# Sums of |w| gathered before one small product, an earlier statistics merge and a split last block in a four-layer convolution kernel

## The chip, the core and the metric

The kernel runs on one core of a Trainium2 chip. The metric is the device time of one execution in microseconds (us). The kernel before took 1045.62 us, the median of 10 runs, which lie between 1042.13 and 1047.35 us.

## The reference: what is computed

The input is a batch of 16 images with 256 channels of 28 x 28 pixels, in float32. Four layers follow each other:

```
layer 0: binarised input, 3x3 convolution with sign-like weights, batch norm, residual
layer 1: sign, 3x3 convolution with real weights, norm, gates, then a 1x1 convolution, gates
layer 2: batchnorm -> sign -> conv(w1) -> prelu -> batchnorm -> sign -> conv(w2) -> prelu -> batchnorm -> + x -> prelu
         conv weights are  mean(|w|) * sign(w)
layer 3: attention over the 784 pixels of each image, projection, + x
```

Two things matter here. The three binary convolutions (one in layer 0, two in layer 2) multiply signs by signs, so they are run with the bare signs, and the scale `mean(|w|)` per output channel enters later, in the normalisation. And the batch norm behind each of them needs the mean and variance of every channel over all 16 images, so nothing after it can start before the last image has been convolved.

## The kernel before, in words

**A binary convolution** is the function `sign_layer`. It is called three times: for layer 0 (its statistics are called `l0`, written `l_` in the profile), and for the two convolutions of layer 2 (`l2b` and `l2c`). An image is cut into two halves of 14 rows x 28 columns = 392 pixels, so there are 32 blocks, numbered `j`. For each block TensorE does 18 matmuls (2 groups of input channels x 9 taps), each with its own 128x128 weights (L285). The two halves of the output channels are packed into one number (`PACK` = 4095), and the function `apart` takes them apart again: two passes on ScalarE (L294, L295) and one on VectorE (L296). The function `post` then works on the block: in layer 0 two `bn_stats` on VectorE (L515) and a conversion to int16 on ScalarE (L516); in layer 2 for each half of the channels a PReLU (L1016) and a `bn_stats` (L1017) on VectorE, and a square on ScalarE (L1019) that watches the range.

**The order** is written out by hand in the loop of `sign_layer`, and each engine works through its part of it in that order. Iteration `j` issues: the products of block `j`; on even `j` the signs of the next image on ScalarE (L390, L982); `post` of block `j - 1`; at `j = 30` the early merge of the statistics; the second part of the previous step (`late`); the first part of the next step; `apart` of block `j`. The products may run ahead of the rest by as many blocks as PSUM has tiles for them, which is three (`ps_conv`, bufs=3).

**Steps** are pieces of work for later layers, put between the blocks. In layer 0 they are, from `j = 2`: six `w1_step` (weights of layer 1) alternating with six `add_up` for layer 0's own weights (odd `j`, 3 to 13), then one step for the 1x1 weights, one for constants, and from `j = 16` to 21 six combined steps for the first weights of layer 2. In the first convolution of layer 2 there is a step that starts loads and then, at `j = 3` to 8, six combined steps for the second weights. A combined step takes the signs of a chunk of weights on ScalarE (L231), packs them on VectorE in its late part (L232), and adds up |w|: `add_up` reduces the chunk to 256 sums per partition on VectorE (L239); its late part, `total_up`, sums those over the partitions with two float32 products with a vector of ones on TensorE (L245; four matmuls in the profile) and adds the result to the scale on VectorE (L247 for the first chunk, L249 for the others). The signs go to a tile with one buffer (`sg`; two in layer 0's own).

**Statistics.** `Moments` holds the `bn_stats` of the blocks. Those of the first 29 blocks go to `parts` and are merged by `gather` (L154, L155) in iteration 30; the last three go to `fin`, beside the merged entry, and a second merge (L171) over 21 numbers per channel half gives mean and variance. `norm` turns them into scale and shift.

**Dummy products.** `keep_busy(n)` issues `n` bf16 products of 512 columns on TensorE whose result nobody reads (L371), to keep its clock up. They stand between the layers, in TensorE's order.

A second version of the whole computation (`careful`) is in the program, but is run only when a check of the ranges asks for it.

Of the kernel before, what the change touches and what calls it, by code (L numbers as in the profile page):

```python
# [28 lines left out]
F32 = mybir.dt.float32  # L29
# [10 lines left out]
P = 128  # L40
# [3 lines left out]
HN = N // 2  # L44
HR = S // 2
K9 = 256 * 9
MC = 112
GN, GC = N // 4, MC // 4
NC_ = N // MC
# [27 lines left out]
def forward(ctx: ExitStack, tc: tile.TileContext, d: dict, out: bass.AP, careful: bool):  # L77
# [16 lines left out]
    def pv(name):  # L94
        return vec[:, VECS.index(name), :]
# [15 lines left out]
    for t, c in ((rounding, ROUND), (unrounding, -ROUND)):  # L111
        nc.gpsimd.memset(t, c)

    doubts = const.tile([P, 8 * B + 6], F32, name="doubts")
    nc.gpsimd.memset(doubts, 0.0)

    def vtile(name):
# [99 lines left out]
    def sign_weights(pool, dst, src, total, acc, stage=("st", 2), tmp=None, ab_tag="rn", sg=("sg", 1)):  # L217


        sts = {}  # L220
        tmp = tmp or pool

        def load(k, g):
            if (k, g) not in sts:
                sts[k, g] = load_taps(pool, src, k, g, *stage)

        def sign(k, g):
            st = sts[k, g]
            n = CHUNKS.index((k, g))
            t = tmp.tile([P, 3, 256], BF16, tag=sg[0], name="sg", bufs=sg[1])  # L230
            A.activation(t, st, AF.Sign, saturate=False)  # L231
            return lambda: V.scalar_tensor_tensor(  # L232
                dst[:, n], t[:, :, P:], PACK, t[:, :, 0:P], ALU.mult, ALU.add
            )

        def add_up(k, g):
            st = sts.pop((k, g))
            ab = tmp.tile([P, 256], F32, tag=ab_tag, name="ab", bufs=4 if ab_tag == "rn" else 2)
            V.tensor_reduce(ab, st.rearrange("p t o -> p o t"), AX.X, ALU.add, apply_absolute_value=True)  # L239
            return lambda: total_up(k, g, ab)  # L240

        def total_up(k, g, ab):
            part = acc.tile([P, 2], F32, tag="sm", name="sumabs")
            for mo in range(2):
                T.matmul(part[:, mo:mo + 1], lhsT=ab[:, mo * P:(mo + 1) * P], rhs=ones, start=True, stop=True)  # L245
            if k == 0 and g == 0:
                V.tensor_scalar(total, part, 1.0 / K9, None, ALU.mult)  # L247
            else:
                V.scalar_tensor_tensor(total, part, 1.0 / K9, total, ALU.mult, ALU.add)  # L249

        return [[Step(lambda c=c: load(*c), lambda c=c, f=f: f(*c)) for c in CHUNKS] for f in (sign, add_up)]

# [14 lines left out]
    def sign_layer(pads, w, temp, sign, post, steps, moments, together=1):  # L267

        pss = [None] * 2 * B
        abs_ = [None] * 2 * B

        groups = 2 if careful else 1
        size = 6 // groups

        def products(*js):
            for j in js:
                pss[j] = conv_ps()
            for n, (k, g) in enumerate(CHUNKS):  # L280
                for j in js:
                    for t in range(3):
                        r, c = divmod(3 * g + t, 3)
                        r += HR * (j % 2)
                        T.matmul(  # L285
                            pss[j][:, n // size, :HN].rearrange("p (a b) -> p a b", b=S), lhsT=w[:, n, t, :],
                            rhs=pads[:, j // 2 % 2, k, r:r + HR, c:c + S],
                            start=(n % size == 0 and t == 0), stop=(n % size == size - 1 and t == 2),
                        )

        def apart(j):
            for g in range(groups):
                t, ab, ps = temp("t1"), temp(), pss[j][:, g, :HN]
                A.activation(t, ps, AF.Identity, bias=rounding, scale=1.0 / PACK)  # L294
                A.activation(ab[:, 1], t, AF.Identity, bias=unrounding)  # L295
                V.scalar_tensor_tensor(ab[:, 0], ab[:, 1], -PACK, ps, ALU.mult, ALU.add)  # L296
                if g == 0:
                    abs_[j] = ab
                else:
                    tt(abs_[j], abs_[j], ab, ALU.add)  # L300

        def sign_image(i):

            for r0, r1 in ((0, HR + 1), (HR + 1, S)) if i < together else ((0, S),):
                sign(i, slice(r0, r1), lambda k: inner(pads[:, i % 2], k, r0, r1))

        late = None
        with tc.manual_schedule(engines={ET.PE, ET.Activation, ET.DVE, ET.SP}):
            sign_image(0)
            for j in range(2 * B):  # L310
                if j == 0:
                    products(*range(together))
                elif together <= j:
                    products(j)
                if j % 2 == 0 and j // 2 + 1 < B:
                    sign_image(j // 2 + 1)
                if j > 0:
                    post(j - 1, abs_[j - 1])
                if j == 2 * B - 2:
                    moments.gather()  # L320
                if late:
                    late()
                late = steps.pop(0)() if j >= 2 and steps else None
                apart(j)
            post(2 * B - 1, abs_[2 * B - 1])
        assert not steps and not late

    def inner(pad, k, r0=0, r1=S):
# [8 lines left out]
        V.tensor_scalar(v, a, f, c, ALU.mult, ALU.add)  # L337
        return v


    def halves_moments(name):
        return Moments(name, 2 * B - 3, 3, (2 * B - 3) * HN)

    sf0, sf1, sf2 = vtile("sf0"), vtile("sf1"), vtile("sf2")
    w0 = packed_weights(wpool, tag="wa")
# [13 lines left out]
    with tc.tile_pool(name="ps_conv", bufs=3, space=PSUM) as psc, \  # L359
# [7 lines left out]
        def keep_busy(n):  # L367

            ps = pss.tile([P, 512], F32, tag="sm", name="unused")
            for _ in range(n):  # L370
                tc.keep_in_program_order(T.matmul(ps, lhsT=idle[:, 0:P], rhs=idle, start=True, stop=True))  # L371

        with tc.tile_pool(name="ph1", bufs=1) as ph:
# [20 lines left out]
            def temp(tag=None):  # L394
                if tag:
                    return ph.tile([P, HN], F32, tag=tag, name=tag, bufs=2)
                return ph.tile([P, 2, HN], F32, tag="rn", name="ab", bufs=4)
# [72 lines left out]

            def constants():
                nc.gpsimd.tensor_copy(
                    doubts[:, 8 * B:], vec[:, VECS.index("a1"):VECS.index("a3") + 1, :].rearrange("p i k -> p (i k)")
                )
                v = const.tile([P, 4, 2], F32, name="v_bn")
                for i, bn in enumerate(bns):
# [31 lines left out]
            steps.insert(13, constants)  # L508

            def post0(j, ab):  # L510
                b, h = divmod(j, 2)
                if h == 0:
                    ns[b] = ph.tile([P, 2, N], I16, tag="n", name=f"n{b}", bufs=2)
                for mo in range(2):
                    V.bn_stats(mom.part(j, mo), ab[:, mo])  # L515
                A.copy(ns[b][:, :, h * HN:(h + 1) * HN], ab)  # L516
                if h == 1:
                    nc.gpsimd.dma_start(out=n0d[b], in_=ns[b])

            mom = halves_moments("l0")  # L520
            sign_layer(fpads, w0, temp, sign0, post0, steps, mom, together=2)
            for b in range(2):
                xs[b] = None
# [347 lines left out]

            with tc.manual_schedule(engines={ET.PE, ET.DVE, ET.Activation}):
                sc0, bi0 = norm("l0", mom, pv("g0"), pv("b0"), sf0, first)
                mom.doubt(doubts[:, 0:4 * B])
                zb1 = tt(vtile("zb1"), bi0, pv("a_move"), ALU.add)
                sign1(0, 0)
                enter(0, 1, sc0)
# [89 lines left out]
        with tc.tile_pool(name="ph2", bufs=1) as ph:  # L967
# [4 lines left out]
                shape = [P, 2, HN] if tag == "ab" else [P, HN]  # L972
                return ph.tile(shape, F32, tag=tag, name=tag, bufs=3 if tag == "ab" else 2)

            keep_busy(12)


            order = [B - 3, B - 2, B - 1] + list(range(B - 3))
# [22 lines left out]
            def post2(order, alpha, mom, doubt):  # L1001

                if careful:
                    beta = combine(mom.name + "_beta", alpha, -1.0, 1.0)

                def post(j, ab):
                    i, h = divmod(j, 2)
                    for mo in range(2):
                        y = ab[:, mo]
                        p = pt[order[i]][:, mo, h * HN:(h + 1) * HN]  # L1010
                        if careful:
                            r = temp("t1")
                            A.activation(r, y, AF.Relu, scale=-1.0)
                            V.scalar_tensor_tensor(p, r, beta[:, mo:mo + 1], y, ALU.mult, ALU.add)
                        else:
                            V.scalar_tensor_tensor(p, y, alpha[:, mo:mo + 1], y, ALU.mult, ALU.max)  # L1016
                        V.bn_stats(mom.part(j, mo), p)  # L1017
                    if not careful:
                        A.activation(temp("t2"), ab[:, 0], AF.Square, scale=SAFE**-0.5, accum_out=doubt[:, j:j + 1])  # L1019
                return post  # L1020

            steps = both(*sign_weights(xpool, w2b, d["w2b"], sf2, pss, ("x2", 3), tmp=ph, ab_tag="sums"))
# [1 line left out]
            def first_loads(some=steps[:2]):  # L1024
                for s in some:
                    s.load()

            steps = [first_loads] + load_ahead(steps, 2, now=False)
            mom = halves_moments("l2b")
            sign_layer(fpads, w2a, temp, sign2a, post2(order, pv("a1"), mom, doubts[:, 4 * B:6 * B]), steps, mom)  # L1030

            keep_busy(30)
            sg2, bg2 = norm("l2b", mom, pv("g2"), pv("b2"), sf1)

            mom = halves_moments("l2c")
            sign_layer(
                fpads, w2b, temp, lambda i, rows, out: sign2(pt[i], sg2, bg2, rows, out),
                post2(range(B), pv("a2"), mom, doubts[:, 6 * B:8 * B]), [], mom,
            )

            keep_busy(45)
# [550 lines left out]
```

## Time and profile before

| | |
|---|---|
| median of 10 runs | 1045.62 us |
| the profiled execution's own time | 1043.47 us |
| its span (first to last instruction) | 1041.7 us |
| granted TensorE clock, mean | 0.991 |
| layer 0, to TensorE's first product of layer 1 | 139.3 us |
| layer 1, to the first product of the first convolution of layer 2 | 139.3 to 514.5 us |
| first convolution of layer 2, to the first product of the second | 514.5 to 640.2 us |
| second convolution of layer 2, to the end of its normalisation | 640.2 to 757.1 us |
| attention and output | to 1041.7 us |

In the profile PE is TensorE's matmuls, PEld its weight loads, DVE is VectorE, ACT is ScalarE, POOL is GpSimd and SP the queue that issues most transfers. A group of instructions is named by line, engine, operation and by what it writes and reads. [...] A matmul's end is modelled, and its duration (356 ns) is longer than the distance from one to the next: block 10 to block 31 of the first convolution of layer 2, 396 matmuls, go from 557.18 to 632.13 us, which is 0.189 us each, or 3.41 us for a block.

### The profile page before, as it was taken

How to read it: one execution, taken by the hardware profiler on the slowest of the kernel's cores; microseconds unless marked ns; L12 is line 12 of the kernel's file. 1: busy time of each engine (PE TensorE's matmuls, PEld its weight loads, DVE VectorE, ACT ScalarE, POOL GpSimd, SP SyncE). 2: the span in 40 equal slices, each digit the busy share in tenths (PEclk: the TensorE clock that was granted, in tenths of full speed). 3: DMA queues.
4: the chain of work that ended last, by engine and by line, in shares of the span. 5: the costliest groups of instructions: out<-in, count | busy, mean ns of one | idle time of the engine just before them, and what ended most of it. 6: DMA issues, size and time to landing. Idle time of an engine off the chain costs nothing.

```text
span 1041.7 us, 15026 instructions
## 1 busy us (share of the span) xinstructions
PE 1007.0 (97%) x5667; PEld 827.4 (79%) x5667; DVE 826.1 (79%) x1460; ACT 729.7 (70%) x1189; POOL 139.4 (13%) x147
## 2 busy tenths in 40 slices
PE   7999999999999999999999999999999999999995
PEld 6899979999999999997589997999844444444442
DVE  4987588999999999985688887888865777768765
ACT  7888746777777777775777775777676676766652
POOL 2000100000000000000100000000024344443531
PEclk9999999999999999999899999999999999999998
DMA  9755521222332223100464000000023435344312
GB/s 345 232 190 189 198 78 47 93 78 78 109 109 93 78 78 107 64 32 31 182 256 180 1 1 1 2 1 1 1 35 59 101 86 124 70 118 92 95 63 97
DMA packets 24358, 98.77 MB, mean 95 GB/s; under 512 B 3202, under 2 KB 6980, under 8 KB 24276
## 3 DMA queue, kind: packets, MB, share of 16 engines
q1 hardware_dynamic: 18644, 67.17, 18.4%
q0 software_dynamic: 5632, 30.54, 10.9%
q8 instruction: 47, 0.77, 0.3%
q14 instruction: 35, 0.29, 0.1%
HBM read 65.59 MB, written 32.11 MB: 94 GB/s over the span
## 4 chain that ended last, share of the span: by engine, by line
PE 82%; DVE 9%; ACT 6%; issue 1%; DMA 1%; SPq 0%; POOL 0%; ACTq 0%; POOLq 0%; DVEq 0%
PE cv L614 27%; PE cv L285 23%; PE sc L1218 8%; PE av L1239 8%; PE cv L720 4%; PE mi L1195 4%; PE sm L1281 2%; PE mi L1297 2%; DVE ab L296 1%; ACT ab L295 1%; DVE p L1016 1%; PE unused L371 1%; ACT t L294 1%; PE sm L1239 1%; DVE l_parts L515 1%
## 5 line engine op out<-in xcount | busy, mean ns | idle before, releaser
L285 PE MATMUL cv<-fpads,wpk 128*128 128x392 f32 x1728 | 336.2, 356 | 9.0 <-POOL l_fin L152 7.3
L285 PEld LDWEIGHTS cv<-fpads,wpk 128*128 128x128 f32 x1728 | 327.2, 192 | 11.8 <-POOL l_fin L152 7.3
L614 PE MATMUL cv<-vs,w 128*128 128x392 f32 x1536 | 301.0, 354 | 1.4 <-DVE vs L121 1.4
L614 PEld LDWEIGHTS cv<-vs,w 128*128 128x128 f32 x1536 | 287.0, 190 | 3.1 <-issue 1.8
L1222 ACT ACTIVATE es<-sc 128x784 f32<-128x784 f32 x112 | 87.3, 822 | 41.4 <-PE sc L1218 41.4
L296 DVE SCALAR_TENSOR_TENSOR ab<-ab,cv 128x392 f32<-128x392 f32 x96 | 53.9, 561 | 65.4 <-ACT ab L295 65.1
L1218 PE MATMUL sc<-q,keyswa 64*128 64x392 f32 x448 | 89.9, 513 | 0.9 <-ACT es L1222 0.9
L1016 DVE SCALAR_TENSOR_TENSOR p<-ab,vec 128x392 f32<-128x392 f32 x128 | 79.1, 618 | 2.2
L1239 PE MATMUL av<-es,v 128*64 128x392 f32 x448 | 80.7, 499 | 0.0
L294 ACT ACTIVATE t<-cv,rounding 128x392 f32<-128x392 f32 x96 | 55.4, 577 | 26.9 <-PE cv L285 25.6
L1218 PEld LDWEIGHTS sc<-q,keyswa 64*128 64x128 f32 x448 | 38.9, 186 | 44.0 <-issue 17.1
L1232 POOL TENSOR_TENSOR sum<-sum,es 128x784 f32<-128x784 f32 x32 | 67.3, 2102 | 3.1 <-ACT es L1222 0.6
L1239 PEld LDWEIGHTS av<-es,v 128*64 128x64 f32 x448 | 29.4, 136 | 47.3 <-issue 47.0
L121 DVE TENSOR_TENSOR vs<-pad 128x840 fp32r<-128x840 bf16 (+1 forms) x66 | 64.5, 1001 | 0.1
L295 ACT ACTIVATE ab<-t,unrounding 128x392 f32<-128x392 f32 x96 | 59.8, 623 | 3.2
L1206 DVE COPY keyswa<-mi 64x392 f32<-64x392 f32 x31 | 16.3, 564 | 52.2 <-ACT q L1202 52.2
L760 POOL DMA_DIRECT2D x2d<-x x16 | 8.6, 536 | 359.5 <-DVE x L754 296.9
L1019 ACT ACTIVATE t<-ab 128x392 f32<-128x392 f32 x64 | 33.5, 523 | 26.6 <-DVE ab L296 26.6
L720 PE MATMUL cv<-z,fw 128*128 128x392 f32 x256 | 48.8, 341 | 0.7 <-ACT z L712 0.7
L737 ACT ACTIVATE u<-cv,c_bn,s_bn 128x784 f32<-128x784 f32 x30 | 30.2, 1005 | 24.4 <-PE cv L720 24.4
L720 PEld LDWEIGHTS cv<-z,fw 128*128 128x128 f32 x256 | 45.8, 188 | 1.5 <-ACT z L712 1.3
L1195 PE MATMUL mi<-p,wqk 128*128 128x392 f32 x124 | 45.3, 506 | 0.3 <-PE unused L371 0.2
(275 smaller groups left out, 1500.3 us busy)
## 6 DMA issues: line engine op xcount, KB each, us to landing
xs<-in_x_dram SPq DMA_DIRECT2D x30, 784.0 KB, 4.9
x2d<-x POOLq DMA_DIRECT2D x16, 784.0 KB, 3.6
out_dram<-p SPq DMA_DIRECT2D x15, 784.0 KB, 3.7
p<-x2d POOLq DMA_DIRECT2D x14, 784.0 KB, 6.9
p<-x2d SPq DMA_DIRECT2D x13, 784.0 KB, 6.7
n0d<-n POOLq DMA_DIRECT2D x16, 392.0 KB, 5.0
n<-n0d SPq DMA_DIRECT2D x16, 392.0 KB, 3.1
st<-in_w_dram SPq DMA_DIRECT2D x12, 384.0 KB, 6.2
```

Source lines behind the costliest of these rows:

```text
L121: V.tensor_tensor(o, a, b, op)
L285: T.matmul(pss[j][:, n // size, :HN].rearrange("p (a b) -> p a b", b=S), lhsT=w[:, n, t, :], rhs=pads[:, j // 2 % 2, k, r:r + HR, c:c + S] ...
L294: A.activation(t, ps, AF.Identity, bias=rounding, scale=1.0 / PACK)
L295: A.activation(ab[:, 1], t, AF.Identity, bias=unrounding)
L614: T.matmul(ps.rearrange("p (a b) -> p a b", b=S), lhsT=w[:, k, c, u, mo * P:(mo + 1) * P], rhs=vs[:, b % 2, u, k, :, c:c + S], start=(n == 0),
L720: T.matmul(ps[:, h, :HN], lhsT=w[:, k, mo * P:(mo + 1) * P], rhs=z2[b][:, k, h * HN:(h + 1) * HN], start=(k + i == 0), stop=(k + i == 2),)
L1016: V.scalar_tensor_tensor(p, y, alpha[:, mo:mo + 1], y, ALU.mult, ALU.max)
L1195: T.matmul(ps[:, h, :HN], lhsT=wqk[:, k, :], rhs=x[b][:, k, h * HN:(h + 1) * HN], start=(k == 0), stop=(k == 1))
L1218: T.matmul(ps[:, h, :HN], lhsT=chunk[rows], rhs=qs[b][rows], start=True, stop=True)
L1222: A.activation(e, ps[:, :, :HN], AF.Exp, scale=0.125)
L1232: (V if late else nc.gpsimd).tensor_tensor(sums[b, late], sums[b, late], e, ALU.add)
L1239: T.matmul(ps[64 * h:64 * h + 64, :HN], lhsT=w, rhs=e[:, h, :], start=start, stop=stop)
```

## The change

There are three parts, and one number.

1. The |w| sums of all six chunks are added on VectorE into one tile of 256 columns (the first chunk is reduced straight into it, each other chunk is reduced into its own tile and then added), and only after the last chunk the two small products sum it over the partitions. So each of the three weight sets has one group of small products instead of six, and five additions of 128x256 on VectorE.
2. The early merge of the statistics covers the first 26 blocks and is issued in iteration 27. The later merge then covers the merged entry and seven blocks, 45 numbers.
3. The last block of 14 rows becomes two of 7 rows, 196 pixels each, so that there are 33 blocks; `products`, `apart` and the `post` functions take the rows of a block from a list.
4. The 12 dummy products ahead of layer 2 become 6.

```
+BLOCKS = [(j // 2, HR * (j % 2), HR) for j in range(2 * B - 1)] + [(B - 1, r, HR // 2) for r in (HR, HR + HR // 2)]
+NB = len(BLOCKS)
+EARLY = 26
...
         def add_up(k, g):
             st = sts.pop((k, g))
-            ab = tmp.tile([P, 256], F32, tag=ab_tag, name="ab", bufs=4 if ab_tag == "rn" else 2)
+            if not all_:
+                all_.append(tmp.tile([P, 256], F32, tag="total", name="sums", bufs=1))
+                ab = all_[0]
+            else:
+                ab = tmp.tile([P, 256], F32, tag=ab_tag, name="ab", bufs=4 if ab_tag == "rn" else 2)
             V.tensor_reduce(ab, st.rearrange("p t o -> p o t"), AX.X, ALU.add, apply_absolute_value=True)
-            return lambda: total_up(k, g, ab)
-
-        def total_up(k, g, ab):
+            if ab is not all_[0]:
+                tt(all_[0], all_[0], ab, ALU.add)
+            return total_up if (k, g) == CHUNKS[-1] else lambda: None
+
+        def total_up():
             part = acc.tile([P, 2], F32, tag="sm", name="sumabs")
             for mo in range(2):
-                T.matmul(part[:, mo:mo + 1], lhsT=ab[:, mo * P:(mo + 1) * P], rhs=ones, start=True, stop=True)
-            if k == 0 and g == 0:
-                V.tensor_scalar(total, part, 1.0 / K9, None, ALU.mult)
-            else:
-                V.scalar_tensor_tensor(total, part, 1.0 / K9, total, ALU.mult, ALU.add)
+                T.matmul(part[:, mo:mo + 1], lhsT=all_[0][:, mo * P:(mo + 1) * P], rhs=ones, start=True, stop=True)
+            V.tensor_scalar(total, part, 1.0 / K9, None, ALU.mult)
...
+                    i, r0, rows = BLOCKS[j]
                     for t in range(3):
                         r, c = divmod(3 * g + t, 3)
-                        r += HR * (j % 2)
+                        r += r0
                         T.matmul(
-                            pss[j][:, n // size, :HN].rearrange("p (a b) -> p a b", b=S), lhsT=w[:, n, t, :],
-                            rhs=pads[:, j // 2 % 2, k, r:r + HR, c:c + S],
+                            pss[j][:, n // size, :rows * S].rearrange("p (a b) -> p a b", b=S), lhsT=w[:, n, t, :],
+                            rhs=pads[:, i % 2, k, r:r + rows, c:c + S],
...
-            for j in range(2 * B):
+            for j in range(NB):
...
-                if j == 2 * B - 2:
+                if j == EARLY + 1:
                     moments.gather()
...
-        return Moments(name, 2 * B - 3, 3, (2 * B - 3) * HN)
+        return Moments(name, EARLY, NB - EARLY, EARLY * HN)
...
-            keep_busy(12)
+            keep_busy(6)
```

The remaining lines give the same row ranges to `apart` and the `post` functions, and widen the tile of the range checks from 134 to 138 columns.

## The prediction

> **What bounds the kernel now.** I read the page's chain of waits first (TensorE 82%, VectorE 9%, ScalarE 6%), then who waited for whom on TensorE, then the timeline around the |w| sums and at the ends of the three binary convolutions.
>
> The waits, as the change sees them: TensorE sat 7.3 us ahead of the small products.
>
> ```profile
> PE sumabs L245 <- DVE ab L239: 7.3, 10, 1.4
> ```
>
> The timeline of one combined step in layer 0: signs of weights (L231), `apart` (L294, L295, L296), statistics, packing (L232), then the next signs.
>
> ```profile
> 86.49 1.03 DVE L239 TENSOR_REDUCE ab<-st 128x256 f32<-128x768 f32 x1
> 86.54 0.84 ACT L231 ACTIVATE sg<-st 128x768 bf16<-128x768 f32 x1
> 87.29 0.57 ACT L294 ACTIVATE t<-cv,rounding 128x392 f32<-128x392 f32 x1
> 87.64 0.52 PEld L245 LDWEIGHTS sumabs<-ones,ab 128*128 128x128 f32 x4 [0.41 <-PE cv L285]
> ...
> 87.89 0.62 ACT L295 ACTIVATE ab<-t,unrounding 128x392 f32<-128x392 f32 x1
> ...
> 88.55 0.56 DVE L296 SCALAR_TENSOR_TENSOR ab<-ab,cv 128x392 f32<-128x392 f32 x1 [1.03 <-ACT ab L295]
> 89.14 1.04 DVE L515 BATCH_NORM_STATS2 l_parts<-ab 128x6 f32<-128x392 f32 x2
> ...
> 90.10 0.54 DVE L232 SCALAR_TENSOR_TENSOR wpk<-sg 128x384 fp32r<-128x384 bf16 x1
> 90.56 0.15 DVE L249 SCALAR_TENSOR_TENSOR sf<-sumabs,sf 128x2 f32<-128x2 f32 x1
> 90.63 1.03 DVE L239 TENSOR_REDUCE ab<-st 128x256 f32<-128x768 f32 x1
> 90.67 0.84 ACT L231 ACTIVATE sg<-st 128x768 bf16<-128x768 f32 x1 [0.69 <-DVE wpk L232]
> ```
>
> From signs to signs is 90.67 - 86.54 = 4.13 us, and no member of that ring is on TensorE: 0.75 to L294, 0.60 to L295, 0.66 to L296, 0.59 to the statistics, 0.96 to L232, 0.57 to the next L231. TensorE needs 18 x 0.19 = 3.42 for its block and 0.44 for the small products. It isn't the bound here: it is dragged by the reduction, which ends at 87.52. In the first convolution of layer 2 the ring is 5.46 us long (L296 at 535.79, 541.25, 546.71, 552.16), and TensorE idles more.
>
> The clock, in stretches of 3.41 us there (columns: us, then busy of PE, PEld, DVE, ACT, POOL, granted clock, DMA): after 2.06 us busy of 3.42 it was halved for just such a stretch.
>
> ```profile
> 544.95:548.36 3.41, 2.54 (x15) 2.56 (x16) 2.31 (x4) 2.31 (x5) 0.00 (x0) 1.00 1.02 425
> 548.36:551.78 3.42, 2.06 (x14) 1.73 (x12) 2.74 (x6) 1.59 (x3) 0.00 (x0) 1.00 1.01 420
> 551.78:555.19 3.41, 3.41 (x12) 3.41 (x12) 2.92 (x6) 2.73 (x5) 0.00 (x0) 0.50 1.02 423
> ```
>
> The end of that convolution: the early merge holds VectorE from 629.71, so `apart` of block 30 starts at 631.56 though ScalarE was done at 630.21.
>
> ```profile
> 629.71 1.72 DVE L154 BATCH_NORM_AGGREGATE l2b_fin<-l2b_parts 128x2 f32<-128x174 f32 x2
> 631.47 0.17 DVE L155 TENSOR_SCALAR l2b_fin<-l2b_fin 128x2 f32<-128x2 f32 x1
> 631.56 0.56 DVE L296 SCALAR_TENSOR_TENSOR ab<-ab,cv 128x392 f32<-128x392 f32 x1
> ```
>
> **The change, part by part.** All sums are differences to the profiled execution (1043.47 us; span 1041.7 and 1.8 around it). It is 2.15 under the median, so I add the difference to the median.
>
> *Additions on VectorE, layer 0's own weights (odd j, 3 to 13).* Here the reduction ends just as ScalarE does: 43.16 + 1.02 = 44.18, L295 ends at 44.20, L296 starts at 44.23, and the chain runs on through VectorE (statistics, L249 0.06, `w1_step`). An addition of 128x256 is the row `asm` of L121: 0.43, of which the next instruction overlaps 0.1. So each of the additions of chunks 2 to 6 delays L296 by 0.31; the sixth passes on 0.26 (ScalarE's signs hide 0.05). Five L249 or L247 go at 0.06: 4 x 0.31 + 0.26 - 0.30 = **+1.2**.
>
> *Additions in the combined steps.* VectorE idles 1.03 ahead of L296 (second fence); 0.45 fits. Cost 0; without that idle time ten of them would cost 4.5.
>
> *TensorE's small products.* 15 of 18 groups go, 0.44 each, but the steps where they stood are paced by the rings, so nothing is won there. The last group stays, between the products of blocks 22 and 23 (9 and 10 in layer 2), and now waits for reduction and addition. Queued behind it is everything TensorE has left of the layer, and from there on the chain is TensorE alone. Addition +0.45, less one L249 of 0.06: **+0.37** in layer 0, **+0.34** in layer 2. The transfers keep their places in SP's and POOL's queues.
>
> *The clock at that wait.* Freed of the other waits, TensorE runs ahead until PSUM's three tiles stop it: block j starts when L296 of block j - 3 ends. In layer 2, block 9 starts at 547.3 (L296 of block 6), ends at 550.7, and the last small products come at 557.15: 6.4 us without work, so the clock is halved when block 10 starts. It stays so until a stretch is mostly busy, some 3.4 us (1.7 to 5.1 by the phase), which costs half: **+1.7** (0 to 2.6), passed on whole, since TensorE then bounds 22 blocks. In layer 0, blocks 20 to 22 come early likewise; L296 of block 19 ends at 93.2, block 22 at about 98 by the queue, the wait lasts to 100.5, and with the 0.44 of near-empty products that makes 2.9 us. A stretch loses over 1.4 of it in most phases: **+1.4** (0 to 2.5).
>
> [...]
>
> *Dummy products, 12 to 6.* They end at 514.52, while ScalarE's first signs (L982 from 512.00, 0.73 each with 0.1 overlap) are there at about 513.3 for both channel groups. TensorE's later dummies lie 0.215 apart at full clock: 6 x 0.215 = 1.29, and conv would start at 513.23, about when its data is there. **-1.3**, passed on through the ring. Ends: 0 (if the clock falls) and -1.3.
>
> *Earlier merge.* 156 numbers at iteration 27 cost 1.6 of VectorE, which gains 3.42 - 2.95 = 0.47 a block in layer 2: absorbed by block 31. In layer 0 VectorE idles 1.8 a block. The last merge grows from 21 to 45 numbers: (902 - 246) / 153 = 4.3 ns each, +0.1 for the one on the path.
>
> *The split block.* No fp32r product of 196 columns is in the trace. Weight loads of 128 columns alone follow each other at 0.11 (four in 0.52, one of them 0.19); a product of 392 takes 0.19. Lower end 0.098 (half of 0.196), upper end 0.354, the float32 rate (L1195, 8 matmuls in 2.83; a product is two of them, at half the columns each). I take 0.11, the row with the same weights and few columns. Then TensorE ends 36 x 0.11 - 3.42 = 0.54 later. VectorE's instruction of 196 columns is L1269: 360 against 625, so 0.265 less each; ScalarE's loses 0.17 (L1173, 1037 to 703 for 392). End of the first convolution of layer 2: without the merge, L296 of block 30 at 630.25, VectorE free at 633.12, quarter one's L296 there, its square on ScalarE at 633.46, quarter two's L294 at 633.93, L295 634.38, L296 634.87, last statistics end 636.53, mean and variance at 636.94 instead of 637.69: **-0.75**. The second convolution has the same end: **-0.75**. In layer 0 the merge hid already; quarter two's L294 waits for the int16 copy of quarter one and starts at 132.36, L296 at 133.30, result 134.59 instead of 134.67: **-0.1**. The 30 dummies behind end 0.54 later and still ahead of the next product.
>
> Sum: 1.2 + 0.37 + 1.4 - 0.1 + 0.34 + 1.7 - 1.3 - 0.75 - 0.75 = **+2.1**, so 1045.6 + 2.1 = 1047.7.
>
> **Rivals.**
>
> *TensorE's queue sets the steps after all* (faster). For it: the chain runs through the small products, 0.60 + 0.38 + 4 x 0.58 in layer 0 and 0.58 + 0.51 in layer 2. Against it: the ring adds up to 4.13 without them. If true, 2.9 and 0.65 go, and TensorE never idles long enough to lose its clock: 2.1 - 2.9 - 0.65 - 3.1 = -4.5, 1041.1. It is faster by the bound once TensorE keeps its clock (-3.1), layer 2 gains its 0.65 and the ring of layer 0 falls under 4.05 us (six steps, -0.45).
>
> *A product of 196 columns costs as much as one of 392* (0.19). TensorE's end comes 3.4 later in each convolution; the tails become +2.4, +1.9 (dummies now end last) and +1.05: 2.1 + 1.6 + 5.35 = +9.1, 1054.7.
>
> *It costs the float32 rate* (0.354). TensorE ends 9.3 later; tails +8.3, +7.8, +6.95: +26.7, 1072. [...]
>
> *The clock holds*: 2.1 - 3.1 = -1.0, 1044.6; it belongs to the likeliest case's own range, 1044.6 to 1049.7 (both losses at their ends).
>
> **How the numbers follow.** Likeliest case 0.70, TensorE's queue 0.12, 0.19 a product 0.06, 0.354 a product 0.12. 0.2% is 2.1 us, about what a measurement of this kernel tells from no change. The likeliest case lies on that bound: 0.37 of its 0.70 above it, 0.30 within, 0.03 below. Slower 0.37 + 0.18 = 0.55, same 0.30, faster 0.15. The range 1041 to 1056 leaves out the float32 rate (0.12) and about half of the case around 1041.1 (0.06).
>
> **What would show it.** Right: L296 in the combined steps still 4.13 and 5.46 apart; in layer 0's odd steps 0.3 more; one `sumabs` group per layer with several us idle ahead of it, and a clock of 0.5 just behind; L154 no longer ahead of block 30; 18 products of a quarter in 2.0 us; conv of layer 2 right behind the signs. Wrong: shorter rings, quarters of 3.4 us or more, no halving.

## The result, and the profile after

The changed kernel takes 1049.14 us (median of 12 runs, 1047.68 to 1050.29) against 1045.63 us for the kernel before (40 runs, 1042.13 to 1048.06): a ratio of 1.0036, with a 95% interval of 1.0026 to 1.0046, so 2.7 to 4.8 us slower. The prediction was 1047.7 us, a change of +2.1. The profiled execution of after took 1048.38 us (span 1046.6, mean clock 0.983); that of before took 1043.47 (span 1041.7, clock 0.991).

Line numbers have moved: the binary products are L293 now, `apart` is L303, L304 and L305, the reduction is L247, the small products are L255, the dummies L379, and the additions are recorded at L125 under the tile `sums`.

**One thing has to be taken off before two profiles are compared: the start.** When the first images land, and how fast the first products go, differ from execution to execution. These lines are from the timeline of after: the signs of the second pair of image parts, and the first block's end on VectorE.

```profile
7.74 0.91 ACT L398 ACTIVATE fpads<-xs 128x364 fp32r<-128x364 f32 x2 [1.22 <-DMA xs<-in_x_dram]
...
18.77 0.56 DVE L305 SCALAR_TENSOR_TENSOR ab<-ab,cv 128x392 f32<-128x392 f32 x1 [4.61 <-ACT ab L304]
```

In before the same two stand at 7.39 and 17.80, and in the ten profiles of this study they lie between 7.39 and 9.12, and between 17.59 and 20.65, with no pattern in what was changed. So the stages below are counted from the first block's end (L296 in before, L305 in after), and the last one ends with TensorE's last product. What is called the first scores are the attention's first products into the tile `sc` (`sc<-p,wqk`, L1195 in before, L1203 in after).

| stage, us | before | after | difference |
|---|---|---|---|
| layer 0, to the first product of layer 1 | 121.48 | 124.76 | +3.28 |
| layer 1, to the first product of layer 2 | 375.24 | 373.98 | -1.26 |
| first convolution of layer 2 | 125.64 | 127.41 | +1.77 |
| second convolution, to the first scores of the attention | 121.46 | 121.25 | -0.21 |
| attention and output | 272.31 | 272.67 | +0.36 |
| sum | 1016.13 | 1020.07 | +3.94 |

The sum agrees with the measured ratio, 0.36% of 1046 or 3.8 us.

**Who waits for whom on TensorE.** Lines of that view of after: engine, line and tile, what it waited for, us in total, times, longest.

```profile
PE sumabs L255 <- DVE sums L125: 11.5, 3, 6.0
...
PE cv L293 <- DVE ab L305: 4.7, 5, 1.1
```

Ten waits of at most 1.4 us have become three, of up to 6.0. There are fewer, and they cost more. The second line is of TensorE waiting for VectorE to free a PSUM tile, which it now does five times; before has no such row.

**Layer 0's odd steps.** VectorE in one of them in before, where L296 starts right behind the reduction, and then in two of them in after, with the addition in between:

```profile
43.16 1.02 DVE L239 TENSOR_REDUCE ab<-st 128x256 f32<-128x768 f32 x1
...
44.23 0.56 DVE L296 SCALAR_TENSOR_TENSOR ab<-ab,cv 128x392 f32<-128x392 f32 x1
```

```profile
36.12 1.02 DVE L247 TENSOR_REDUCE ab<-st 128x256 f32<-128x768 f32 x1
37.17 0.42 DVE L125 TENSOR_TENSOR sums<-sums,ab 128x256 f32<-128x256 f32 x1
37.52 0.55 DVE L305 SCALAR_TENSOR_TENSOR ab<-ab,cv 128x392 f32<-128x392 f32 x1
...
45.73 0.56 DVE L305 SCALAR_TENSOR_TENSOR ab<-ab,cv 128x392 f32<-128x392 f32 x1
```

L305 of the odd blocks is 8.22 us apart (37.52, 45.73, 53.95), where L296 of before was 7.96 apart (36.27, 44.23, 52.19): 5 x 0.26 = 1.3 us.

**The one group of small products that is left.** In before the last group in the first convolution of layer 2 starts without a wait:

```profile
556.75 0.58 PE L245 MATMUL sumabs<-ones,ab 128*128 128x1 f32 x4
...
557.18 1.00 PE L285 MATMUL cv<-fpads,wpk 128*128 128x392 f32 x4
```

The timeline of after, in layer 0 and then in the first convolution of layer 2:

```profile
101.09 1.02 DVE L247 TENSOR_REDUCE ab<-st 128x256 f32<-128x768 f32 x1
...
102.15 0.43 DVE L125 TENSOR_TENSOR sums<-sums,ab 128x256 f32<-128x256 f32 x1
...
102.63 0.61 PE L255 MATMUL sumabs<-ones,sums 128*128 128x1 f32 x4 [1.84 <-DVE sums L125]
...
103.10 0.58 PE L293 MATMUL cv<-fpads,wpk 128*128 128x392 f32 x1
...
559.56 0.42 DVE L125 TENSOR_TENSOR sums<-sums,ab 128x256 f32<-128x256 f32 x1
560.04 1.01 PE L255 MATMUL sumabs<-ones,sums 128*128 128x1 f32 x4 [6.03 <-DVE sums L125]
560.91 0.67 PE L293 MATMUL cv<-fpads,wpk 128*128 128x392 f32 x1
```

TensorE stands idle for 1.84 and 6.03 us, since it had run ahead as far as PSUM let it, and block 23 (block 10 in layer 2) is queued behind the products. In layer 2 the four small matmuls then take 1.01 us instead of 0.61 and block 10 starts 0.87 behind them, not 0.43 as in before (556.75 to 557.18): they ran at half clock already (0.50 from 557.22 us on).

The first of the three waits, 3.60 us ahead of the products for layer 0's own weights (70.52 us), costs nothing that can be seen. Two stretches behind it are at half clock as well (69.12 to 75.94 us, 0.50), and yet L305 of blocks 14 to 22 comes 1.26 to 1.30 us later than in before, counted from the first block's end: as much as run 1 below has there, with 14 dummies in that wait. The rings set the pace of these blocks, not TensorE.

**The clock at that wait.** Stretches of 3.41 us of after, laid along the steps of the granted clock (columns: us, then busy of PE, PEld, DVE, ACT and POOL, with numbers of instructions; granted clock; DMA):

```profile
99.84:103.25 3.41, 1.57 (x11) 1.22 (x10) 2.74 (x6) 2.69 (x5) 0.00 (x0) 0.99 0.40 164
103.25:106.67 3.42, 3.42 (x11) 3.42 (x12) 2.67 (x9) 3.27 (x5) 0.54 (x1) 0.51 0.28 62
106.67:110.08 3.41, 3.41 (x19) 3.40 (x19) 2.08 (x4) 2.67 (x4) 0.00 (x0) 1.00 0.76 285
...
553.81:557.22 3.41, 0.20 (x2) 0.00 (x0) 2.68 (x6) 3.38 (x6) 0.00 (x0) 1.00 1.01 419
557.22:560.63 3.41, 0.59 (x3) 0.59 (x3) 2.70 (x6) 2.24 (x5) 0.00 (x0) 0.50 1.02 423
560.63:564.05 3.42, 3.42 (x12) 3.42 (x13) 3.31 (x8) 2.79 (x6) 0.00 (x0) 0.51 0.08 30
564.05:567.46 3.41, 3.41 (x20) 3.40 (x19) 3.20 (x10) 2.52 (x5) 0.00 (x0) 1.00 0.01 2
```

Count the matmuls: a full stretch holds 18 to 20 at full clock, and 11 or 12 behind the wait. From the start of block 23 to the first dummy behind the convolution TensorE needs 32.77 us instead of 30.73; 0.62 of that belongs to the quarters, which is what the two blocks of 7 rows are called (below), so 1.42 was lost to the clock. In layer 2, from block 10, it is 76.91 against 74.98: 1.31 lost.

**The ends of the two convolutions of layer 2.** The timeline of after, first convolution, VectorE from block 30 on:

```profile
635.29 0.56 DVE L305 SCALAR_TENSOR_TENSOR ab<-ab,cv 128x392 f32<-128x392 f32 x1 [0.28 <-ACT ab L304]
...
638.17 0.34 DVE L305 SCALAR_TENSOR_TENSOR ab<-ab,cv 128x196 f32<-128x196 f32 x1
...
640.00 0.34 DVE L305 SCALAR_TENSOR_TENSOR ab<-ab,cv 128x196 f32<-128x196 f32 x1
...
640.38 0.42 DVE L1024 SCALAR_TENSOR_TENSOR p<-ab,vec 128x196 f32<-128x196 f32 x1
640.84 0.37 DVE L1025 BATCH_NORM_STATS2 l2b_fin<-p 128x6 f32<-128x196 f32 x1
...
642.05 0.36 DVE L175 BATCH_NORM_AGGREGATE l2b_mv<-l2b_fin 128x2 f32<-128x45 f32 x1
642.45 0.16 DVE L125 TENSOR_TENSOR l2b_v<-l2b_mv,l2b_e 128x2 f32<-128x2 f32 x1
```

The merge no longer stands ahead of block 30: its L305 comes 1.28 us behind its `t` (L303) instead of 2.59. But two quarters follow where one half did, 2.88 and then 1.83 us later, and from the last one to the variance it is 2.45. From block 30's `t` to the variance it is 8.44 instead of 8.72.

And at the end of the second convolution, in before (variance, first product of the attention) and in after (last dummies, variance, first product):

```profile
755.43 0.16 DVE L121 TENSOR_TENSOR l2c_v<-l2c_mv,l2c_e 128x2 f32<-128x2 f32 x1
...
759.54 1.86 PE L1195 MATMUL mi<-p,wqk 128*128 128x392 f32 x4 [0.22 <-PE unused L371]
```

```profile
759.12 5.56 PE L379 MATMUL unused<-idle 128*128 128x512 bf16 x25
...
759.49 0.15 DVE L125 TENSOR_TENSOR l2c_v<-l2c_mv,l2c_e 128x2 f32<-128x2 f32 x1
...
764.78 0.57 PE L1203 MATMUL mi<-p,wqk 128*128 128x392 f32 x1
```

Here the variance is ready 0.70 earlier than in before (114.57 us behind the start of the convolution instead of 115.27), but the dummies run until 764.68, and the first product of the attention starts 5.29 us behind the variance instead of 4.11. The gain stays in front of TensorE's queue.

### The profile page after: what moved, and what is told of

Same layout as the page of the kernel before. It is cut to its first block, busy times and chain, and to the rows that moved or that the text cites. A ratio compares the mean times of both kernels' runs of the same rounds, so it can differ in the third digit from the quotient of the medians.

```text
span 1046.6 us, 15039 instructions
## 1 busy us (share of the span) xinstructions
PE 1004.9 (96%) x5655; PEld 828.2 (79%) x5655; DVE 833.1 (80%) x1473; ACT 733.2 (70%) x1200; POOL 139.8 (13%) x147
## 4 chain that ended last, share of the span: by engine, by line
PE 81%; DVE 9%; ACT 7%; issue 1%; DMA 1%; SPq 0%; ACTq 0%; DVEq 0%
PE cv L622 27%; PE cv L293 21%; PE sc L1226 8%; PE av L1247 7%; PE mi L1203 4%; PE cv L728 4%; PE sm L1289 2%; PE unused L379 2%; PE mi L1305 2%; DVE ab L305 2%; DVE l_parts L523 2%; ACT ab L304 1%; ACT t L303 1%; PE sm L1247 1%; DVE p L1024 1%
## 5 line engine op out<-in xcount | busy, mean ns | idle before, releaser
L293 PE MATMUL cv<-fpads,wpk 128*128 128x392 f32 (+1 forms) x1782 | 340.1, 354 | 13.2 <-POOL l_fin L156 7.3
L293 PEld LDWEIGHTS cv<-fpads,wpk 128*128 128x128 f32 x1782 | 334.0, 194 | 18.6 <-POOL l_fin L156 7.3
L305 DVE SCALAR_TENSOR_TENSOR ab<-ab,cv 128x392 f32<-128x392 f32 (+1 forms) x99 | 54.3, 549 | 62.0 <-ACT ab L304 61.8
L1024 DVE SCALAR_TENSOR_TENSOR p<-ab,vec 128x392 f32<-128x392 f32 (+1 forms) x132 | 80.0, 606 | 2.3
L303 ACT ACTIVATE t<-cv,rounding 128x392 f32<-128x392 f32 (+1 forms) x99 | 56.4, 569 | 28.4 <-PE cv L293 26.6
L125 DVE TENSOR_TENSOR vs<-pad 128x840 fp32r<-128x840 bf16 (+1 forms) x66 | 64.5, 1002 | 0.1
L304 ACT ACTIVATE ab<-t,unrounding 128x392 f32<-128x392 f32 (+1 forms) x99 | 60.8, 614 | 3.3
L1027 ACT ACTIVATE t<-ab 128x392 f32<-128x392 f32 (+1 forms) x66 | 34.0, 516 | 26.3 <-DVE ab L305 26.2
L1203 PE MATMUL mi<-p,wqk 128*128 128x392 f32 x124 | 45.1, 506 | 0.1
```

The lines of the kernel that those rows point to most:

```text
L293: T.matmul(pss[j][:, n // size, :rows * S].rearrange("p (a b) -> p a b", b=S), lhsT=w[:, n, t, :], rhs=pads[:, i % 2, k, r:r + rows, c:c + S],
L1203: T.matmul(ps[:, h, :HN], lhsT=wqk[:, k, :], rhs=x[b][:, k, h * HN:(h + 1) * HN], start=(k == 0), stop=(k == 1))
```

## The experiments

Theory A is that of the prediction: what costs is the additions, and the one late group of small products with the clock that falls behind it (0.51 and 0.50 in after); the split and the earlier merge are worth little. Rival B: the sums are neutral, and the split and the merge cost. For the comparisons with before, the runs of before made beside each run are used (1044.74 us median of 26 for the first four, 1044.32 us of 15 for the others), which lie about 1 us under the 1045.6 that most expectations start from. The last column is from one profile each and counts from the first block's end, as in the table above.

| | us, median | ratio to before, interval | profile, us to before |
|---|---|---|---|
| after | 1049.14 | 1.0036, 1.0026 to 1.0046 | +3.94 |
| 1: TensorE kept busy ahead of the late products | 1043.95 | 0.9999, 0.9986 to 1.0012 | +0.57 |
| 2: the sums alone | 1053.61 | 1.0084, 1.0065 to 1.0104 | +8.84 |
| 3: everything but the sums | 1044.10 | 0.9999, 0.9985 to 1.0012 | -1.18 |
| 4: late products put far behind their sums | 1040.41 | 0.9957, 0.9942 to 0.9972 | -3.73 |
| 5: after, unsplit | 1048.95 | 1.0037, 1.0023 to 1.0050 | +3.27 |
| 6: after, 39 dummies instead of 45 | 1048.40 | 1.0036, 1.0025 to 1.0048 | +4.84 |
| 7: 4, unsplit, 39 dummies | 1040.55 | 0.9965, 0.9952 to 0.9978 | -4.47 |
| 8: 7, layer 0's additions on GpSimd | 1038.43 | 0.9948, 0.9936 to 0.9960 | -5.23 |

**1. Does the clock at the late wait cost what it seems to?** The wait stays as it is; TensorE is only given dummies ahead of the late products (14 for layer 0's own weights, 8 and 26 for the two sets of layer 2).

```
         def total_up():
+            keep_busy(fill)
             part = acc.tile([P, 2], F32, tag="sm", name="sumabs")
```

> The changed kernel with dummy bf16 products (14, 8 and 26 of them, 3.0, 1.7 and 5.6 us at 0.215 each) on TensorE right ahead of the last small products of the three weight sets, where it sits idle. Theory A (the |w| sums cost 1.3 by the additions in layer 0's odd steps, 0.6 by the later last small products, and 3.2 by the clock halved behind that wait): the three halvings at 69, 103 and 557 us are gone, TensorE gains 1.4 in layer 0 and 1.75 in layer 2, so the time is 3.2 under the changed kernel and within 1 us of the kernel before (1044.6 to 1047). Rival B (the sums pay for themselves, and the split block with its larger merge is what costs): the clock behind the wait is beside the point, time as the changed kernel, 1049.

Measured: 1043.95 us, the time of before. The stretches of this run in the first convolution of layer 2, TensorE's 6 us of idling filled:

```profile
552.67:556.08 3.41, 3.34 (x16) 1.56 (x17) 2.67 (x6) 3.38 (x6) 0.00 (x0) 1.00 1.01 418
556.08:559.50 3.42, 3.01 (x16) 1.54 (x15) 2.71 (x6) 2.18 (x5) 0.00 (x0) 1.00 1.01 420
559.50:562.91 3.41, 3.41 (x19) 3.39 (x19) 3.31 (x8) 2.85 (x6) 0.00 (x0) 1.00 0.08 29
```

The clock stays at 1.00, the small products take 0.61 again, the first convolution of layer 2 takes 125.67 instead of 127.41, and layer 0 123.32 instead of 124.76. So 1.4 and 1.7 us of after are the clock, with the small products that ran at half of it. Theory A holds; B had no place for this.

**2. The sums alone.** The kernel before with the `sign_weights` of after; no earlier merge, no split, 12 dummies.

```
 (in before.py)
-            return lambda: total_up(k, g, ab)
+            if ab is not all_[0]:
+                tt(all_[0], all_[0], ab, ALU.add)
+            return total_up if (k, g) == CHUNKS[-1] else lambda: None
...
```

> The kernel before with the new |w| sums alone. Theory A: +1.3 + 0.6 + 3.2 = +5 us, 1050.7 (1049 to 1052); the halved clock behind the last small products as in the changed kernel. Rival B: between -1 and +1 us, 1045.6.

Measured: 1.0084, some 8.8 us slower: the direction of A, and more than its 5. The trace shows where the rest is in one of the slower executions (1055.53 us; the six lie between 1051.89 and 1055.64). Stretches of this run in layer 2:

```profile
556.37:559.78 3.41, 1.41 (x8) 1.05 (x6) 2.72 (x6) 2.82 (x5) 0.00 (x0) 1.00 1.02 421
559.78:563.19 3.41, 0.00 (x0) 0.00 (x0) 3.34 (x6) 2.30 (x6) 0.00 (x0) 0.51 1.01 423
563.19:566.61 3.42, 2.80 (x10) 2.80 (x11) 2.68 (x6) 2.73 (x7) 0.00 (x0) 0.50 0.44 180
566.61:570.02 3.41, 3.41 (x12) 3.41 (x11) 3.38 (x10) 2.51 (x5) 0.00 (x0) 0.50 0.00 0
...
648.53:651.94 3.41, 1.69 (x9) 1.45 (x9) 0.85 (x6) 2.38 (x4) 0.00 (x0) 1.00 0.00 0
651.94:655.36 3.42, 3.42 (x13) 3.42 (x12) 0.00 (x0) 2.02 (x3) 0.00 (x0) 0.51 0.02 5
```

Here the stretches of the clock lay so that the wait straddled two of them, and the clock was halved for three: the loss behind block 10 is 2.31 us instead of 1.31. The start of the second convolution fell into another halved stretch (its first block's end comes 1.40 later than in before), and layer 2's first product came 4.09 us behind the first signs, where it was 2.52 in before with the same 12 dummies and 1.22 in after with 6; the author put that down to one more such stretch. Layer 0 costs +3.23, as in after. So the sum of this profile is 3.23 + 0.68 + 3.42 + 1.47 + 0.04 = 8.84. In the first convolution the 3.42 are 0.75 up to block 10, where after has 0.74, 2.31 behind it, and 0.37 at the old merge ahead of block 30; the 3.23 of layer 0 hold 1.3 of additions. What lies beyond the sums' own cost is in this profile, by the author's estimate, mostly halved stretches that fell where before had none; how much of it the faster executions had, no trace shows.

**3. Everything but the sums.** After, with the `sign_weights` of before.

> The changed kernel with the old |w| sums, so that the earlier merge, the split block and 6 dummies are left of the change. Theory A: -1.3 for the dummies and -0.75 for the three ends, -2.0 us, 1043.6 (1042.5 to 1044.6). Rival B: +3 us or more, 1048.6.

Measured: 0.9999 (0.9985 to 1.0012), so neither A's -2.0 nor B's +3. The profile gives -1.18: layer 0 +0.27, the way to layer 2 -0.92, the two convolutions -0.29 and -0.16. B falls. Of A the wait and the clock stand, but the ends, to which the prediction gave -1.6 in all and this expectation -0.75, bring 0.2 at most: that was still open, and is what runs 5 and 6 are for.

**4. The wait taken away by moving who waits.** The late products of all three weight sets are issued two or more blocks behind the last sum, as steps of their own (for this the second set has its own tile of sums).

```
-            return total_up if (k, g) == CHUNKS[-1] else lambda: None
+            return lambda: None
...
+            nothing = lambda: (lambda: None)
+            steps += [nothing, nothing, lambda: total0, lambda: total1]
...
+            steps = [first_loads] + load_ahead(steps, 2, now=False) + [nothing, nothing, lambda: total2]
```

> The changed kernel with the last small products issued three blocks later (behind the products of blocks 25, 26 and, in layer 2, 12; the two sums of layer 0 in tiles of their own), so that TensorE never waits for an addition. Theory A: the clock's 3.2 and the 0.6 go, and TensorE may run ahead of the rings: in layer 0 block 24 starts when its image is signed (2.0 earlier than in the kernel before), in layer 2 block 10 some 4 earlier than in the kernel before; behind that TensorE is the bound, so 1045.6 + 3.5 - 3.8 - 2.0 - 4.0 = 1039.3 (1038.5 to 1042). A variant C of it: ScalarE and VectorE hold the blocks behind the rings too, the running ahead is worth nothing, and 3.8 go: 1045.3. Rival B: as the changed kernel, 1049.

Measured: 1040.41 us, 0.9957 (0.9942 to 0.9972): faster than both kernels, as A expected, though 4.5 us under the runs of before and not 6.3. Variant C, in which the running ahead is worth nothing (1045.3), falls. Lines of its timeline, and stretches of it around the place where after waited:

```profile
111.89 0.50 PE L255 MATMUL sumabs<-ones,sums 128*128 128x1 f32 x4
...
566.10 0.50 PE L255 MATMUL sumabs<-ones,sums 128*128 128x1 f32 x4
```

```profile
550.68:554.09 3.41, 1.30 (x8) 0.94 (x6) 2.71 (x5) 2.97 (x5) 0.00 (x0) 1.00 1.01 419
554.09:557.51 3.42, 3.42 (x11) 3.29 (x12) 3.32 (x7) 2.32 (x5) 0.00 (x0) 0.50 1.01 422
557.51:560.92 3.41, 3.41 (x18) 3.06 (x17) 2.69 (x5) 2.72 (x7) 0.00 (x0) 1.00 0.39 158
```

No wait stands at the small products any more. The clock is halved once here too (0.50 from 554.09 us), behind a stretch with 1.30 us of work, since the ring of 5.46 us still leaves TensorE idle; but TensorE is ahead of VectorE then, and the lost time is covered: L305 of blocks 9 to 17 comes 2.9 us apart on average (46.43 to 69.84 us after the convolution's start), at VectorE's pace, where before goes at TensorE's 3.41 from block 14 on. The convolution takes 123.50 us instead of 125.64.

**5. What is the split worth?** After with 32 blocks.

```
-BLOCKS = [(j // 2, HR * (j % 2), HR) for j in range(2 * B - 1)] + [(B - 1, r, HR // 2) for r in (HR, HR + HR // 2)]
+BLOCKS = [(j // 2, HR * (j % 2), HR) for j in range(2 * B)]
```

> After, with the last half image convolved whole again (32 blocks; the statistics still aggregated at 26, small products as after). Theory D (the split costs more than it saves at the ends, the earlier merge alone is the gain): from block 30's t to l2b_v takes 8.44 us in after; whole, block 31's L305 comes 2.87 behind block 30's (1.28 + 2.87 = 4.15) and the tail of before is 3.26 + 0.1, so 7.5: -0.9. The second convolution of layer 2: -0.6, as the dummies behind it end that much earlier with TensorE. Layer 0: 9.96 instead of 10.19 from block 30's L305 to the next layer: -0.2. Sum -1.7: 1047.4 us (1046.4 to 1048.4). Rival E (the split shortens the tails, as half a block less lies behind the last product): tails go back to before's lengths, +0.3 and +0.2, layer 0 -0.2: 1049.4 us.

Measured: 1.0037 (1.0023 to 1.0050), not to be told from after by time. In the profile every end is shorter without the split: block 30's `t` to the variance takes 8.09 instead of 8.44 and 8.30 instead of 8.50, layer 0's end 10.10 instead of 10.19, and with TensorE's earlier end the scores of the attention come 0.58 earlier. Direction of D, but well under half of its size: the whole profile is 0.67 below that of after. D had put block 31's L305 2.87 us behind block 30's, the distance in before, where VectorE was catching up behind the merge. Here it is 3.40 (117.77 and 121.17 us behind the start), a whole block of TensorE, which now ends last.

**6. The dummies behind the second convolution.**

```
-            keep_busy(45)
+            keep_busy(39)
```

> After, with 39 instead of 45 dummies behind the second convolution of layer 2. Theory F (the dummies end at 764.68 and hold the first product of the attention, L1203 at 764.78, so that the 0.7 won ahead of l2c_v is lost there): L1203 starts 4.6 us behind l2c_v instead of 5.29, as in before (4.11 with the table load in the same place), so -0.7: 1048.4 us; read from the trace, as the time can't tell it. Rival G (the product waits for VectorE's residuals, which end then anyway): 5.29 stays, 1049.1 us. If the clock is halved by the shorter filling, up to +1.7.

By time not to be told from after (1.0036). In its timeline:

```profile
761.78 0.15 DVE L125 TENSOR_TENSOR l2c_v<-l2c_mv,l2c_e 128x2 f32<-128x2 f32 x1
...
765.88 1.86 PE L1203 MATMUL mi<-p,wqk 128*128 128x392 f32 x4 [0.20 <-PE unused L379]
```

The first product comes 4.10 us behind the variance again, as in before: F holds, and it was the dummies that had kept it. (Run 7, where 39 dummies end still earlier, has 4.11 too; there the product waits 0.60 us for the tile `p` on VectorE, not for the dummies.) The scores come 0.52 earlier; the rest of the 1.19 goes to the additions of the residual on VectorE (tile `p`), for which the scores then wait. The same run shows the cost of the late wait where the stretches of the clock lie elsewhere: behind the late products 2.48 us were lost in layer 0 (0.50 and 0.51 from 103.54 to 110.36 us) and 2.30 in layer 2 (0.50 and 0.51 from 557.51 to 567.75), where after lost 1.42 and 1.31, which is why its profile stands at +4.84.

**7 and 8. A better version.** Run 7 is run 4 with 32 blocks and 39 dummies; run 8 also moves layer 0's five additions to GpSimd.

```
-                tt(all_[0], all_[0], ab, ALU.add)
+                (add or V.tensor_tensor)(all_[0], all_[0], ab, ALU.add)
...
+            signs, sums_, total0 = sign_weights(ph, w0, d["w0"], sf0, pss, ("yu", 6), sg=("t1", 2), add=nc.gpsimd.tensor_tensor)
```

> The late total of the earlier run (1040.4 us), with the last half image whole and 39 dummies behind the second convolution of layer 2. Theory D and F: -0.9, -0.2 and from the second convolution's end -1.0 (the first product of the attention then comes 1.2 earlier than in before, where 0.2 is won with split and 45): 1038.3 us (1037 to 1040). Rival E: the split is what keeps the ends short, +0.3 + 0.2: 1040.9 us or more.

> The same, with the additions of layer 0's own |w| on GpSimd (it idles there; its addition of 128x784 in the attention takes 2.10 us, so 128x256 about 0.7). Theory A: L305 of the odd steps comes 7.96 apart again instead of 8.22, 5 x 0.26 = 1.3 less: 1037.0 us. Rival H (VectorE and GpSimd hold one another up, or GpSimd's transfers of images wait behind the additions): VectorE loses 0.7 instead of 0.31 each, 6 x 0.4: 1040.7 us.

Run 7 measured 1040.55 us (0.9965), which is not below run 4's 1040.41; its profile is 0.74 below run 4's (first convolution 123.16 instead of 123.50, second 120.54 instead of 121.25, layer 0 0.17 less, the attention 0.51 more), a third of what was expected, in the first convolution for the reason of run 5. By time run 7 does not decide between D with F and E (1040.9 or more); only the profile leans to D. Run 8 measured 1038.43 us (0.9948), 2.1 under run 7's median, with intervals that overlap; its profile is 0.75 below run 7's. One of its odd steps in layer 0:

```profile
42.82 1.03 DVE L247 TENSOR_REDUCE ab<-st 128x256 f32<-128x768 f32 x1
43.95 0.56 DVE L305 SCALAR_TENSOR_TENSOR ab<-ab,cv 128x392 f32<-128x392 f32 x1
44.01 0.73 POOL L249 TENSOR_TENSOR sums<-sums,ab 128x256 f32<-128x256 f32 x1 [4.94 <-DVE ab L247]
```

L305 of the odd blocks is 7.91 apart on average (28.10 to 67.63 over five), even less than before's 7.96, and layer 0 takes 120.29 us instead of 121.70: A's 1.3 is recovered, and rival H falls. L305 takes the same 0.56 us beside the addition (at 43.95) as without it (at 41.27). Of the versions run this has the lowest median.

## Why the prediction was right, and where it was not

The mechanism was right: the small products were never what paced the steps, and freeing TensorE of them turned the small waits of each weight set into a long one; two of the three were not hidden, and the clock fell behind them (to 0.51 in layer 0, 0.50 in layer 2). The size was about half of what the profile shows, +2.1 of +3.94. Term by term, as the two profiles have it:

| step of the prediction | predicted, us | measured, us |
|---|---|---|
| additions in layer 0's odd steps | +1.2 | +1.31 |
| additions in the combined steps | 0 | 0 (L305 4.14 and 5.46 apart, as before) |
| last small products later | +0.37, +0.34 | +0.31, +0.30 |
| halved clock behind that wait | +1.4, +1.7 | +1.42, +1.31 |
| the small products themselves at half clock | none | +0.43 in layer 2 |
| dummies, 12 to 6 | -1.3 | -1.30 at the signs, -1.26 for the stage |
| end of layer 0 | -0.1 | +0.24 |
| ends of layer 2's convolutions | -0.75, -0.75 | -0.28, -0.21 |
| attention | 0 | +0.36 |
| sum | +2.1 | +3.94 |

**What was right.** The place and the size of the odd-step additions (they lie between the reduction and L305, with nothing to hide them); the zero for the combined steps, where the 1.03 us of idle time took the addition; the dummies; and the halving in both layers. A product of 196 columns with 128 columns of weights was unknown: 36 of them take 0.62 us more than the 18 whole ones (3.41), 4.03 / 36 = 0.112 us each, where the row of weight loads had given 0.11. The rival of 0.19 a product and that of the float32 rate fall with that. The fp32r products of before all have 392 columns; the 0.112 for half of them, beside 0.189, is the first row that bears on the size. The lower end, "half of 0.196", was an estimate: 0.196 is L614's busy time by product (301.0 us over 1536), and the halving is shown by no row; the products of L285 in before are 0.189 apart.

**What was luck.** That 1.42 and 1.31 us were lost to the clock, so near to +1.4 and +1.7, is luck in part. The prediction gave layer 0 2.9 us of wait and near-empty products; 1.84 and 0.61 were measured. And behind the same waits run 6 lost 2.48 and 2.30, a play of about 1 us that the ranges of the two terms (0 to 2.5 and 0 to 2.6) allowed for.

**What was wrong: the ends.** The step "End of the first convolution of layer 2 ... -0.75" carried the first half well: block 30's L305 comes 1.31 earlier (predicted 1.31), the quarters' 2.88 and 1.83 apart (2.87 and 1.75). Its last piece was mis-sized: from the last quarter's L305 to the variance it is 2.45 us, not 2.07. L1024 and L1025 shrink by 0.21 each (0.63 to 0.42, 0.57 to 0.36), while the row of L1269 had given 0.265, and the aggregation of 45 numbers takes 0.35 where that of 21 took 0.24, twice. Layer 0's end, +0.24 in place of -0.1, has the same tail on VectorE: from the last L305 to the variance it is 1.53 us, not 1.29. For the second convolution the prediction said "The second convolution has the same end"; its variance did come 0.70 earlier, but behind it stand 45 dummies, which had ended just 0.2 us ahead of the first product of the attention and now end 0.6 later (counted from the start of the convolution) with the quarters. The sentence "The 30 dummies behind end 0.54 later and still ahead of the next product" was true for 30 of them and never asked for the 45: run 6 shows that it was they. These three ends are +1.35 of the 1.8 that are missing from the sum.

**The rest.** The small products at half clock (+0.43) belong to the same halving, one instruction earlier than the prediction looked. The 0.36 of the attention hold the clock again: the last projection took 5.43 us instead of 4.60, which is more than the whole difference, and 2.24 us of TensorE's last work fell into a halved stretch (1035.08 to 1038.49), of which before has only 0.19 (from 1033.10). It could have gone either way with the place of these stretches; run 8, whose end falls likewise (2.03 us of work from 1025.13 to 1028.54, at 0.51), has +0.58 there.

**The rivals.** That TensorE's queue set the steps: no, the rings are what they were. That the clock holds: it did not, and run 1, which made it hold by filling (1.00 where after had 0.50), is in keeping with the price: it came out at 0.9999 of before (0.9986 to 1.0012), where that case gave -1.0 us.

## What to carry to other kernels

When work is taken off an engine that wasn't the bound, ask where its next wait falls: small waits spread over many steps can be cheaper than one wait at the end. Here the ten waits of before, 1.4 us at most, lay in steps that the rings paced; behind two of the three of after, 1.84 and 6.03 us long, the clock was at half as well, and 1.42 and 1.31 us were lost to it. A product that needs a long chain of sums should be issued some blocks after the sums, not right behind them; that alone turned +0.36% into -0.43%. And whoever changes the work around a block of dummies has to check when the dummies end: here they held back 0.5 us, which only the profile of run 6 shows.

## What the runs showed of the hardware that was not expected

**The granted clock changed stretch by stretch, behind stretches with little work.** In all ten profiles the granted clock changes on a grid of 3.413 us (in after the steps at 69.08 and 564.01 us lie 145 of them apart), whose position differs from execution to execution: a step of before falls at 551.78 us, one of after at 557.19. Of the stretches of that grid at full clock between 20 and 1024 us, all 29 in which TensorE was busy for less than 1.75 us were followed by one at 0.5; of the 14 with 1.75 to 2.25 us, 5 were; of those with more, none. Not one of the 29 was without any work. This is a count and not a bound: a stretch of run 7 that ends past 1024 us (1022.86 to 1026.27, 1.71 us of work) was followed by one at 1.00. In layer 0 of after the wait of 1.84 us left 1.57 us of work in its stretch (99.84 to 103.25); the next was at 0.51, and 1.42 us were lost.

**The same wait has several prices.** Behind the late products 1.42, 1.44, 1.44 and 2.48 us were lost in layer 0, and 1.31, 1.33, 2.31 and 2.30 in layer 2, in the four kernels that have that wait (after and runs 5, 2 and 6, in this order). That goes with the number of halved stretches there: one in layer 0 in after and run 5, two in run 6; two in layer 2 in after and run 5, three in runs 2 and 6. A halved stretch with 3.41 us of work was the last one each time in before and after, as the prediction had it, but not always: in run 6 the one from 103.54 us was at 0.50 with 3.41 us of work, and the next was at 0.51. A single profile doesn't give the price of such a wait, only one draw of it.

**The start scatters more than most of the effects.** The first block's end lay between 17.59 and 20.65 us in the ten profiles. The landing of the first images is not all of it: run 8 and after sign the second pair of image parts at the same 7.74 us, and yet run 8's first block ends 1.18 us earlier. Between 11.40 and 15.40 us TensorE worked on 22 products there and on 16 in after, with both busy throughout, and the column of the granted clock has 1.00 for both; what made the difference was not shown. Where no halved stretch falls differently, a stage agrees to 0.1 us between profiles (layer 1 takes 373.95 to 373.98 us in after and runs 4, 7 and 8); the spans can't be compared like that.
